# A perceiver layer on one core: one more slice in a seven-product down projection, and its products moved behind the next slice's gate and up products

## The chip, the cores and the metric

One core of a Trainium2 chip runs the whole program in one launch. The metric is the device time of an execution in microseconds (us). TensorE is called PE in the profile, VectorE DVE, ScalarE ACT, GpSimd POOL, and SyncE, which here only issues transfers, SP.

## The reference

The layer has three blocks on 256 tokens of width 512: cross attention with sigmoid scores over a context of 25088 tokens, causal self attention with 16 heads, and a feed-forward block. All is fp32. Only the last one is touched:

```
gu = x @ shared_gate_up_w
shared = _silu(gu[:, :Is]) * gu[:, Is:] @ shared_down_w
shared = shared * jax.nn.sigmoid(x @ shared_gate_w)
...
w, idx = jax.lax.top_k(probs, TOP_K)
...
act = _silu(gu_e[..., :I]) * gu_e[..., I:]
out_e = jnp.einsum('eci,eih->ech', act, expert_down_w)
...
return (y + shared).reshape(B, S, H)
```

The shared expert's inner width is 1024, an expert's 256; each token goes to 8 of 64 experts, weighted.

## The kernel before

**Stages.** Cross attention runs over 66 groups of context tokens and takes most of the time; self attention and the feed-forward block follow. In the last one the shared expert is cut into four slices ("s", 0) to ("s", 3) of inner width 256, so that a slice has the shape of an expert: gate and up weights of 512 x 512, down weights of 256 x 512. After the slices come the eight experts with most tokens, ("e", 0) to ("e", 7), each on all 256 tokens, and smaller work for experts with few tokens.

**One slice or expert.** gate_up (L1205) makes two PSUM banks by gate_up_products (L1187): 8 matmuls 128x256 for the gate, 8 for the up half. Sigmoid on ScalarE and two multiplies on VectorE (L1216 to L1218) make the hidden values hT, 256 x 256. down (L1347) then multiplies hT with the down weights, in one of two ways:

- Plain: for each of two token tiles two matmuls 128x512 (L1356), and one VectorE operation (L1365) that multiplies the result by the tokens' weights and adds it to what is summed so far: x2 (the residual) for ("s", 0), which thereby starts y, and y itself for the others.
- By seven products: the members of SEVEN (L803), which are slices 1 to 3 and experts 0 to 6, have their hT multiplied by the token weights first (L1220; a row of weights, broadcast to all partitions). hT and the down weights are each seen as 2 x 2 blocks. Four sums of blocks of hT are made on VectorE (S) and four of blocks of the weights on GpSimd (T), both at L1283 in sums_for_seven; then seven matmuls 128x256 (L1299 in down_by_seven), which go into two pairs of PSUM banks kept from the first member to the last. The first member starts the accumulation and the last one ends it; then add_seven (L1310) forms y from the seven totals in eleven VectorE operations.

**Order around the change.** run (L1369) issues gate_up of a slice, then down of the one before it, then what the table "between" has for this step: counted (token counts and the ranking of experts) after slice 0, load_first (weights of experts 0 to 2) after slice 1, permuted (the step pp, perm and pw_wt) after slice 2. So TensorE has: slice 0 gate and up, slice 1 gate and up, slice 0 down, slice 2 gate and up, slice 1 down, slice 3 gate and up, slice 2 down, slice 3 down, expert 0 gate and up. Between the two halves of slice 1's products, turn_weights (L1177) turns the token weights; GpSimd's queue stores them in DRAM (L1182) and reads one row back to all partitions (L1183), the row that slices multiply by. A scheduler orders the instructions of an engine, save those marked in_turn, which keep the program's order.

**Buffers and queues.** Weights of slices and experts share three buffers for gate and up and three for down (wpool), loaded through SP's queue, which waits in order: slice 3's take slice 0's, expert 0's take slice 1's, and so on. The S sums alternate between two rooms (the tiles x1 and x, no longer needed), by the member's place in SEVEN; the T sums have two buffers. Four PSUM banks, taken in turn by bank, serve gate and up halves, plain down products and the small matmuls of counted, turn_weights and permuted: each is used again four calls later.

Of the kernel before, what the change touches and what calls it, by code (L numbers as in the profile page):

```python
# [11 lines left out]
ALU = mybir.AluOpType  # L12
AX = mybir.AxisListType

P = 128
# [6 lines left out]
def tile_perceiver_layer(  # L22
# [25 lines left out]
    nc = tc.nc  # L48

    T, D = x.shape  # L50
# [10 lines left out]
    NI = I // P  # L61
# [445 lines left out]
    for i in range(2):  # L507
        t = cpool.tile([P, NT_SUMS, WIDTH + 2], F32, tag=f"T{i}", name=f"T_{i}", bufs=1)
# [174 lines left out]
    for line in RESULTS.strip().splitlines():  # L683
        to, x_, op, y_ = line.split()
        a_, b_, o_ = result(x_), result(y_), result(to)
        n = widths[to] = min(widths[x_], widths[y_])
        assert to not in ("c01", "c11") or n == WIDTH
        if to[0] == "c" and to[2] != "1":
            n = WIDTH - 2
# [83 lines left out]
    def bank(name):  # L773
        turns[1] += 1
        return apart(name) if turns[1] % 4 == 0 else among_three(name)
# [15 lines left out]
    NS = IS // I  # L791
    WHOLE = 8
# [6 lines left out]

    SEVEN = [("s", k) for k in range(1, NS)] + [("e", k) for k in range(WHOLE - 1)]  # L803
    weights = {}
    scales = {}
    late = ctx.enter_context(tc.tile_pool(name="late", bufs=1))
# [28 lines left out]
    def spread(tile_, row):  # L835
        return tile_.unsqueeze(1), weights_of_tokens[row, :].partition_broadcast(P)

    def load_expert(k, gu=None, dn=None, by=SP):
# [16 lines left out]
        queue.dma_start(dn, e_down[bass.ds(e, 1)].rearrange("o (c p) f -> p (o c) f", p=P))  # L855
        if ("e", k) in SEVEN:
            sc = scales["e", k] = scale_rooms[1 + k % 3]
# [73 lines left out]
    x2 = late.tile([P, NT, D], F32, tag="x2", name="x2")  # L931
# [200 lines left out]
    wsh = wt[:, :, E : E + 1]  # L1132
# [44 lines left out]
    def turn_weights():  # L1177
        pt = bank("pt_wt")
        for t in range(NT):
            nc.tensor.transpose(pt[0 : E + 1, t * P : (t + 1) * P], wt[:, t, :], ident)  # L1180
        nc.vector.tensor_copy(wT, pt[0 : E + 1, :T])
        nc.gpsimd.dma_start(weights_of_tokens, wT)  # L1182
        nc.gpsimd.dma_start(*spread(scale_rooms[0], slice(E, E + 1)))  # L1183
        for k in range(1, NS):
            scales["s", k] = scale_rooms[0]

    def gate_up_products(n, halves, lo, hi, mark=lambda ins: ins):  # L1187
        gu, _ = weights[n]
        for half, ph in enumerate(halves):
            if half > 0 and n == SEVEN[0]:  # L1190
                turn_weights()
            for f in range(NI):
                col = half * I + f * P
                for c in range(ND):
                    mark(
                        nc.tensor.matmul(  # L1196
                            ph[:, f * T + lo : f * T + hi],
                            lhsT=gu[:, c, col : col + P],
                            rhs=fT[:, c, lo:hi],
                            start=(c == 0),  # L1200
                            stop=(c == ND - 1),
                        )
                    )

    def gate_up(n, tiles_done=None):  # L1205

        nm = f"{n[0]}{n[1]}"
        if tiles_done is None:
            halves = [bank(f"ph_{nm}_{half}") for half in range(2)]
            gate_up_products(n, halves, 0, T)  # L1210
        else:
            halves = tiles_done
        pg, pu = halves
        hT = hidden.tile([P, NI, T], F32, tag="hT", name=f"hT_{nm}")
        hf = hT.rearrange("p f t -> p (f t)")
        nc.scalar.activation(hf, pg, AF.Sigmoid)  # L1216
        nc.vector.tensor_mul(hf, pg, hf)
        nc.vector.tensor_mul(hf, pu, hf)  # L1218
        if n in SEVEN:
            nc.vector.tensor_mul(hT, hT, scales.pop(n).unsqueeze(1).to_broadcast([P, NI, T]))  # L1220
            sums_of[n] = sums_for_seven(n, hT)
        return hT

# [20 lines left out]
        "p2 s3 b11",  # L1246
    )
    SUMS_OF_SEVEN = """
        y00 y00 + p0
        u1 p0 + p5  # L1250
        y00 y00 + p1
        u3 u1 + p4
        y01 y01 + u3
        y01 y01 + p2
        u2 u1 + p6
        u0 u2 - p3
        y10 y10 + u0
        u3 u2 + p4
        y11 y11 + u3
    """  # L1260
    HALF = D // 2
    sums_of = {}
    seven = []

    def block(n, hT, dn, s, t, nm):
        i, k = nm[1:2], nm[2:3]
        if nm[0] == "a":
            return hT[:, int(k), int(i) * P : (int(i) + 1) * P]
        if nm[0] == "b":
            return dn[:, int(i), int(k) * HALF : (int(k) + 1) * HALF]  # L1270
        return (s if nm[0] == "s" else t)[:, int(i), :]

    def sums_for_seven(n, hT):
        _, dn = weights[n]

        where = "x" if SEVEN.index(n) % 2 else "x1"
        s_ = act.tile([P, 4, P], F32, tag=where, name=f"s_{n[0]}{n[1]}")
        t_ = work.tile([P, 4, HALF], F32, tag="tokT", name=f"t_{n[0]}{n[1]}")
        for engine, text in ((nc.gpsimd, T_OF_SEVEN), (nc.vector, S_OF_SEVEN)):
            for line in text.strip().splitlines():  # L1280
                to, x_, op, y_ = line.split()
                f = engine.tensor_add if op == "+" else engine.tensor_sub
                made = f(*(block(n, hT, dn, s_, t_, nm) for nm in (to, x_, y_)))  # L1283
                if engine is nc.gpsimd:
                    in_turn(made)
        return s_, t_

    def product_of_seven(nm):
        i = int(nm[1])
        return seven[i // 4][:, i % 4 // 2, i % 2 * HALF : (i % 2 + 1) * HALF]  # L1290

    def down_by_seven(n, hT):
        _, dn = weights.pop(n)
        s_, t_ = sums_of.pop(n)
        if not seven:
            seven.extend(banks(f"seven_{i}") for i in range(2))
        for text in PRODUCTS_OF_SEVEN:
            nm, lhs, rhs = text.split()
            nc.tensor.matmul(  # L1299
                product_of_seven(nm),  # L1300
                lhsT=block(n, hT, dn, s_, t_, lhs),
                rhs=block(n, hT, dn, s_, t_, rhs),

                start=(n == SEVEN[0] and nm in ("p0", "p3", "p4", "p6")),
                stop=(n == SEVEN[-1] and nm in ("p1", "p2", "p5", "p6")),
            )
        if n == SEVEN[-1]:
            add_seven()

    def add_seven():  # L1310
        u = work.tile([P, 4, HALF], F32, tag="tok", name="u_seven")
        p5 = u[:, 0, :]
        nc.scalar.copy(p5, product_of_seven("p5"))

        def named(nm):
            if nm[0] == "y":
                return y[:, int(nm[1]), int(nm[2]) * HALF : (int(nm[2]) + 1) * HALF]
            if nm[0] == "u":
                return u[:, int(nm[1]), :]
            return p5 if nm == "p5" else product_of_seven(nm)  # L1320

        for line in SUMS_OF_SEVEN.strip().splitlines():
            to, x_, op, y_ = line.split()
            f = nc.vector.tensor_add if op == "+" else nc.vector.tensor_sub
            f(named(to), named(x_), named(y_))
# [4 lines left out]
    first = [pair[:, half, :] for half in range(2)]  # L1330
    route(0)
    gate_up_products(("s", 0), first, 0, P, in_turn)
    transposed_tile(fT, fn, 1, "fn", 2, two=True)
    route(1)
    gate_up_products(("s", 0), first, P, T, in_turn)
    for t in range(NT):
        choose(t)
# [3 lines left out]
    y = late.tile([P, NT, D], F32, tag="y", name="y")  # L1341
# [5 lines left out]
    def down(n, hT, parts=WIDE_PARTS):  # L1347
        if n in SEVEN:
            down_by_seven(n, hT)
            return  # L1350
        _, dn = weights.pop(n)
        nm = f"{n[0]}{n[1]}"
        for t, lo, hi in parts:
            pd = bank(f"pd_{nm}_{t}_{lo}")[:, 0 : hi - lo]
            for f in range(NI):
                nc.tensor.matmul(  # L1356
                    pd,
                    lhsT=hT[:, f, t * P : (t + 1) * P],
                    rhs=dn[:, f, lo:hi],
                    start=(f == 0),  # L1360
                    stop=(f == NI - 1),
                )
            w = wsh[:, t, :] if n[0] == "s" else wso[:, t, n[1] : n[1] + 1]
            so_far = x2 if n == ("s", 0) else y
            nc.vector.scalar_tensor_tensor(  # L1365
                y[:, t, lo:hi], pd, w, so_far[:, t, lo:hi], ALU.mult, ALU.add
            )

    def run(names, between, last=WIDE_PARTS):  # L1369

        pending = None
        for i, n in enumerate(names):
            hT = gate_up(n, first if n == ("s", 0) else None)
            if pending is not None:
                down(*pending)
            pending = (n, hT)
            if i in between:
                between[i]()
        down(*pending, last)


    order = late.tile([1, E], mybir.dt.int32, tag="order", name="order")
# [1 line left out]
    wso = late.tile([P, NT, E], F32, tag="wso", name="wso")  # L1384
# [261 lines left out]
    def remaining(lo):  # L1646
# [33 lines left out]
        last=LAST_PARTS,  # L1680
# [66 lines left out]
```

## Time and profile before

| | us |
|---|---|
| median of three runs | 778.94 |
| lowest and highest | 778.67, 779.83 |
| the profiled execution | 778.86 |
| its span (first to last instruction) | 777.1 |
| PE busy, DVE busy, POOL busy in it | 766.2, 557.9, 184.5 |

The profiled execution's own time is 1.76 us longer than its span. The granted PE clock was 0.999 of full speed. The feed-forward block's slices lie between 622 us and 661 us of the span.

How to read it: the profile has one row for each instruction that an engine ran, with the start (us from the span's start), the length, the line of the kernel and the tiles it wrote and read. An fp32 matmul of the program is two rows. "PEld" are the weight loads, which overlap the matmuls. The chain that ended last follows the work back from the last instruction, at each step to what released it. A DMA's time to landing runs from its issue until its data are there. An engine's wait is idle time of that engine, put down to what ended it.

### The profile page before, as it was taken

The numbers are of one execution on the slowest core, as the hardware profiler recorded it, in microseconds if no ns is written. First come the engines' busy times: TensorE is split into PE (matmuls) and PEld (weight loads), VectorE is DVE, ScalarE is ACT, GpSimd is POOL, SyncE is SP. The second block draws the span as 40 slices with busy tenths as digits, with TensorE's granted clock in tenths as the row PEclk, the third lists the DMA queues.
The fourth block names the chain that finished last, engine by engine and source line by source line (L and its number), as shares of the span: only waits on it lengthen the run. The fifth ranks groups of instructions, "written<-read, shape, count | busy, mean of one in ns | idle before, by whom it ended". The sixth has DMA issues, their size and how long they took to land.

```text
span 777.1 us, 12400 instructions
## 1 busy us (share of the span) xinstructions
PE 766.2 (99%) x4072; PEld 623.7 (80%) x4072; DVE 557.9 (72%) x1638; ACT 201.4 (26%) x486; POOL 184.5 (24%) x346
## 2 busy tenths in 40 slices
PE   8999999999999999999999999999999999999996
PEld 5888888888888888888888888888676588887574
DVE  5978878878888788788788888887756583523223
ACT  4222222222222222222222222222345320110110
POOL 3222322222223223222222232232123032131200
PEclk9999999999999999999999999999999999999999
DMA  9999999999787787787887887850430043599600
GB/s 251 284 233 249 256 237 272 232 225 216 180 208 181 188 206 176 203 200 173 207 194 168 213 190 184 211 134 2 138 107 2 0 145 102 165 323 390 233 1 31
DMA packets 154902, 141.98 MB, mean 183 GB/s; under 512 B 9238, under 2 KB 114339, under 8 KB 154832
## 3 DMA queue, kind: packets, MB, share of 16 engines
q1 hardware_dynamic: 154000, 140.41, 71.0%
q8 instruction: 34, 0.56, 0.3%
q10 hardware_dynamic: 672, 0.52, 0.2%
q0 software_dynamic: 160, 0.20, 0.2%
q14 instruction: 36, 0.29, 0.1%
HBM read 140.52 MB, written 0.59 MB: 182 GB/s over the span
## 4 chain that ended last, share of the span: by engine, by line
PE 96%; DVE 2%; ACT 0%; DMA 0%; POOL 0%; issue 0%; ACTq 0%
PE xacc L579 37%; PE pk L360 22%; PE pz L378 11%; PE ph_e L1196 7%; PE seven L1299 4%; PE ph_s L1196 3%; PE pw L941 2%; PE pa L877 2%; PE ph_few L1571 1%; PE ps L967 1%; PE ptp L1018 1%; PE po_few L1602 1%; PE pf L1548 1%; PE py L738 1%; PE pd_few L1616 1%; DMA x_sb<-in_x 0%
## 5 line engine op out<-in xcount | busy, mean ns | idle before, releaser
L579 PE MATMUL xacc<-T,S 128*128 128x172 f32 (+2 forms) x912 | 185.5, 308 | 0.0
L360 PE MATMUL pk<-cT,wkT_sb 128*128 128x384 f32 x512 | 175.5, 486 | 0.0
L579 PEld LDWEIGHTS xacc<-T,S 128*128 128x128 f32 x912 | 152.7, 190 | 20.3
L360 PEld LDWEIGHTS pk<-cT,wkT_sb 128*128 128x128 f32 x512 | 97.2, 190 | 54.3
L546 POOL TENSOR_TENSOR T<-ctx 128x172 f32<-128x172 f32 x65 | 31.7, 487 | 385.4 <-PE xacc L579 379.7
L324 DVE STREAM_TRANSPOSE cT<-quarters 128x1536 f32<-128x1536 f32 x64 | 113.2, 1770 | 0.2 <-issue 0.2
L546 DVE TENSOR_TENSOR T<-ctx 128x172 f32<-128x172 f32 (+1 forms) x262 | 113.3, 433 | 0.0
L546 DVE TENSOR_TENSOR S<-zT 128x128 f32<-128x128 f32 x196 | 56.2, 287 | 72.5 <-ACT zT L387 72.5
L378 PE MATMUL pz<-qT,kT 128*128 128x256 f32 x392 | 106.1, 379 | 0.7 <-ACT kT L369 0.7
L387 ACT ACTIVATE zT<-pz 128x256 f32<-128x256 f32 (+1 forms) x131 | 64.1, 489 | 114.1 <-PE pz L378 114.1
L579 PE MATMUL xacc<-T,zT 128*128 128x173 f32 (+1 forms) x396 | 90.0, 309 | 0.0
L579 PE MATMUL xacc<-ctx,S 128*128 128x172 f32 x392 | 78.5, 309 | 0.0
L369 ACT ACTIVATE kT<-pk,bk 128x384 f32<-128x384 f32 (+1 forms) x66 | 38.0, 577 | 147.0 <-PE pk L360 147.0
L546 DVE TENSOR_TENSOR S<-zT,S 128x128 f32<-128x128 f32 x325 | 76.1, 283 | 0.0
L556 ACT COPY T<-ctx 128x170 f32<-128x170 f32 (+1 forms) x130 | 43.1, 333 | 125.5 <-PE xacc L579 121.2
L546 POOL TENSOR_TENSOR T<-ctx,T 128x170 f32<-128x170 f32 (+1 forms) x130 | 72.3, 574 | 2.2 <-PE xacc L579 2.2
L378 PEld LDWEIGHTS pz<-qT,kT 128*128 128x128 f32 x392 | 68.6, 190 | 4.8 <-ACT kT L369 1.3
L546 DVE TENSOR_TENSOR T<-ctx,T 128x172 f32<-128x172 f32 x195 | 65.5, 361 | 8.2 <-PE xacc L579 1.5
L579 PEld LDWEIGHTS xacc<-T,zT 128*128 128x128 f32 x396 | 66.4, 190 | 0.1
L579 PEld LDWEIGHTS xacc<-ctx,S 128*128 128x128 f32 x392 | 62.8, 190 | 0.0
L579 PE MATMUL xacc<-ctx,zT 128*128 128x170 f32 (+1 forms) x264 | 59.5, 307 | 0.0
L1196 PE MATMUL ph_e<-fT,gu 128*128 128x256 f32 x256 | 57.8, 381 | 0.3 <-DVE rank L1504 0.3
(281 smaller groups left out, 770.0 us busy)
## 6 DMA issues: line engine op xcount, KB each, us to landing
ctx<-in_context SPq DMA_DIRECT2D x65, 768.0 KB, 5.4
quarters<-in_context SPq DMA_DIRECT2D x256, 192.0 KB, 6.5
gu<-in_e_gate_up SPq DMA_DIRECT2D x12, 1024.0 KB, 8.9
dn<-in_e_down SPq DMA_DIRECT2D x11, 512.0 KB, 6.8
gu_s<-in_s_gate_up SPq DMA_DIRECT2D x8, 512.0 KB, 6.2
a_wqT<-in_a_wqT SPq DMA_DIRECT2D x1, 2048.0 KB, 13.3
a_wout<-in_a_woutT SPq DMA_DIRECT2D x1, 2048.0 KB, 10.3
dn_s<-in_s_down SPq DMA_DIRECT2D x4, 512.0 KB, 8.1
```

Source lines behind the costliest of these rows:

```text
L324: in_turn(nc.vector.transpose(new_turned(g), q.rearrange("p b (c r) -> p c b r", r=R)))
L360: nc.tensor.matmul(pk, lhsT=w[:, c, :], rhs=cT[:, c, 0 : n // R, :].rearrange("p b r -> p (b r)"), start=(c == 0), stop=(c == ND - 1),)
L369: in_turn(nc.scalar.activation(kT[:, 0:n], pk, AF.Identity, bias=bk_sb))
L378: nc.tensor.matmul(pz[:, i * T : (i + 1) * T], lhsT=kT[:, at : at + P], rhs=qT, start=True, stop=True,)
L387: nc.scalar.activation(zT[:, blocks[0] : blocks[-1] + 1, :].rearrange("p j t -> p (j t)"), pz[:, 0 : len(blocks) * T], AF.Sigmoid, scale=1 ...
L546: in_turn(f(o_, a_, b_))
L556: in_turn(nc.scalar.copy(named[to][:, 0:n], named[x_][:, 0:n]))
L579: nc.tensor.matmul(banks_of_products[i][:, cols], lhsT=named[lhs], rhs=named[rhs][:, 0:n],  start=i not in opened, stop=(g == G - 1 and last),
L877: nc.tensor.matmul(pa[:, 0 : hi - lo], lhsT=a_wqT_sb[:, c, e * P : (e + 1) * P], rhs=anT[:, c, lo:hi], start=(c == 0), stop=(c == ND - 1),)
L941: nc.tensor.matmul(pw[t], lhsT=oT[:, e, t * P : (t + 1) * P], rhs=a_wout_sb[:, e, :], start=(e == 0), stop=(e == NE - 1),)
L1196: nc.tensor.matmul(ph[:, f * T + lo : f * T + hi], lhsT=gu[:, c, col : col + P], rhs=fT[:, c, lo:hi], start=(c == 0), stop=(c == ND - 1),)
L1299: nc.tensor.matmul(product_of_seven(nm), lhsT=block(n, hT, dn, s_, t_, lhs), rhs=block(n, hT, dn, s_, t_, rhs),  start=(n == SEVEN[0] and ...
```

## The change

Slice 0 becomes a member of SEVEN: its hT is multiplied by the row of token weights, and it takes the seven products in place of the four plain matmuls and the two updates of y. Since that row exists only after slice 1's gate and up products have begun, slice 0's multiply and sums are made after slice 1's own (weigh), and run holds slice 0's products back: no down is issued after slice 1's gate and up, and both slice 0's and slice 1's are issued after slice 2's. The final sums read x2 where they read y, since no plain product starts y any more. Slice 0 is now the member that starts the accumulation.

```diff
-    SEVEN = [("s", k) for k in range(1, NS)] + [("e", k) for k in range(WHOLE - 1)]
+    SEVEN = [("s", k) for k in range(NS)] + [("e", k) for k in range(WHOLE - 1)]
...
-        for k in range(1, NS):
+        for k in range(NS):
             scales["s", k] = scale_rooms[0]
...
-            if half > 0 and n == SEVEN[0]:
+            if half > 0 and n == ("s", 1):
                 turn_weights()
...
-        if n in SEVEN:
-            nc.vector.tensor_mul(hT, hT, scales.pop(n).unsqueeze(1).to_broadcast([P, NI, T]))
-            sums_of[n] = sums_for_seven(n, hT)
+        if n in SEVEN and n != ("s", 0):
+            weigh(n, hT)
         return hT
+
+    def weigh(n, hT):
+        nc.vector.tensor_mul(hT, hT, scales.pop(n).unsqueeze(1).to_broadcast([P, NI, T]))
+        sums_of[n] = sums_for_seven(n, hT)
...
-        y00 y00 + p0
+        y00 x00 + p0
...
-        y01 y01 + u3
+        y01 x01 + u3
...
-        y10 y10 + u0
+        y10 x10 + u0
...
-        y11 y11 + u3
+        y11 x11 + u3
...
-            w = wsh[:, t, :] if n[0] == "s" else wso[:, t, n[1] : n[1] + 1]
-            so_far = x2 if n == ("s", 0) else y
+            w = wso[:, t, n[1] : n[1] + 1]
...
-        pending = None
+        pending = []
         for i, n in enumerate(names):
             hT = gate_up(n, first if n == ("s", 0) else None)
-            if pending is not None:
-                down(*pending)
-            pending = (n, hT)
+            if n == ("s", 1):
+
+                weigh(*pending[0])
+            else:
+                for each in pending:
+                    down(*each)
+                pending = []
+            pending.append((n, hT))
             if i in between:
                 between[i]()
-        down(*pending, last)
+        for each in pending:
+            down(*each, last)
```

More of the change, by code (lines that the diff above doesn't have):

```diff
@@ L1315, in named @@
         def named(nm):
-            if nm[0] == "y":
-                return y[:, int(nm[1]), int(nm[2]) * HALF : (int(nm[2]) + 1) * HALF]
+            if nm[0] in "xy":
+                return (x2 if nm[0] == "x" else y)[:, int(nm[1]), int(nm[2]) * HALF : (int(nm[2]) + 1) * HALF]
             if nm[0] == "u":
@@ L1362, in down @@
                 )
-            w = wsh[:, t, :] if n[0] == "s" else wso[:, t, n[1] : n[1] + 1]
-            so_far = x2 if n == ("s", 0) else y
+            w = wso[:, t, n[1] : n[1] + 1]
             nc.vector.scalar_tensor_tensor(
-                y[:, t, lo:hi], pd, w, so_far[:, t, lo:hi], ALU.mult, ALU.add
+                y[:, t, lo:hi], pd, w, y[:, t, lo:hi], ALU.mult, ALU.add
             )
     def run(names, between, last=WIDE_PARTS):
-        pending = None
+        pending = []
         for i, n in enumerate(names):
             hT = gate_up(n, first if n == ("s", 0) else None)
-            if pending is not None:
-                down(*pending)
-            pending = (n, hT)
+            if n == ("s", 1):
[5 more added lines that the diff above has]
+            pending.append((n, hT))
             if i in between:
                 between[i]()
-        down(*pending, last)
+        for each in pending:
+            down(*each, last)
     order = late.tile([1, E], mybir.dt.int32, tag="order", name="order")
```

## Prediction

> **What bounds the kernel now.** I read the page first: busy time by engine, then the chain that ended last.
>
> ```profile
> PE 766.2 (99%) x4072; PEld 623.7 (80%) x4072; DVE 557.9 (72%) x1638; ACT 201.4 (26%) x486; POOL 184.5 (24%) x346
> ...
> PE 96%; DVE 2%; ACT 0%; DMA 0%; POOL 0%; issue 0%; ACTq 0%
> ```
>
> TensorE is never idle and the chain lies on it: 96% of the span. So a microsecond of TensorE work that disappears is a microsecond of time, provided nothing else becomes late. Next, the same chain in order of time around the edit (start, length, what):
>
> ```profile
> 626.71 3.22 PE ph_s L1196 x14
> 629.93 0.22 PE pt_wt L1180 x2
> 630.15 3.46 PE ph_s L1196 x16
> 633.61 3.43 PE pd_s L1356 x8
> 637.04 6.91 PE ph_s L1196 x32
> 643.95 3.02 PE seven L1299 x14
> 646.97 0.25 PE pp L1433 x2
> ```
>
> Here pd_s is slice 0's down product, ph_s at 637.04 slice 2's gate and up, seven at 643.95 slice 1's down by seven products. TensorE goes from one to the next without a gap. Each fp32 matmul of the program is two rows (four matmuls give x8, seven give x14). Last, the timeline of VectorE and GpSimd in the stretch where the moved work will land:
>
> ```profile
> 637.57 0.14 DVE L1422 CAST active<-left 1x1 int32<-1x1 f32 x1
> 637.60 0.73 POOL L1283 TENSOR_TENSOR t_s<-dn_s,t_s 128x256 f32<-128x256 f32 x1
> 637.64 0.73 DVE L1365 SCALAR_TENSOR_TENSOR y<-pd_s,wt,x 128x512 f32<-128x512 f32 x1
> 638.29 1.27 POOL L1283 TENSOR_TENSOR t_s<-dn_s 128x256 f32<-128x256 f32 x1
> 638.30 0.67 DVE L1220 TENSOR_TENSOR hT_s<-hT_s,wqT 128x512 f32<-128x512 f32 x1
> 639.00 1.44 DVE L1283 TENSOR_TENSOR s_s<-hT_s 128x128 f32<-128x128 f32 x2
> 639.52 0.77 POOL L1283 TENSOR_TENSOR t_s<-t_s,dn_s 128x256 f32<-128x256 f32 x1
> ...
> 645.43 0.50 DVE L1283 TENSOR_TENSOR s_s<-hT_s 128x128 f32<-128x128 f32 x2
> ```
>
> The same pair of small sums took 0.50 us with GpSimd idle and 1.44 us beside it; GpSimd's add took 1.27 instead of 0.72 when VectorE's multiply of two SBUF operands started beside it. So these two engines take turns.
>
> **The change part by part.**
>
> *Products (removed and added).* Four matmuls 128x512 go (3.43 us), seven 128x256 come (3.02 us, by slice 1's row): **-0.41 us** of TensorE, all on the path. Nothing else on TensorE changes but its order.
>
> A rule against this is in the Trainium skill, "TensorE: Matmul & The Clock Gate", section on the back-to-back issue gap: a sustained stream of weight load and matmul costs 81 ns at 128 columns and 131 ns at 512. Interpolated (my estimate) that is 98 ns at 256, and fourteen short rows would cost 1.31 times eight long ones: +1.1 us instead of -0.41. The trace disagrees: 3.02/14 = 0.216 us and 3.43/8 = 0.429 us, proportional to the columns.
>
> *Order.* Slice 2's gate and up moves up to 633.61 and ends 6.91 later, at 640.52; slice 0's seven products follow, then slice 1's to 646.56, where before they ended at 646.97. What each start needs:
>
> - Slice 2's weights were requested with the first three slices, long before. Its two PSUM banks are now those of the token counts (read at 626.75) and of slice 1's gate half (read by 631.6): free.
> - Slice 1's products start 0.41 us earlier behind a longer queue; their operands are made before slice 0's. No wait.
> - Slice 0's products need its hidden values weighed, four S sums (VectorE) and four T sums (GpSimd). This is the tight place.
>
> *The tight place.* Before, TensorE's weight load for the first of the seven stood at 643.57; it now falls at 643.57 - 3.43 = 640.14, with 0.43 us (3.02/7) per product: the third product (needs the last T sum) at 641.00, the fourth (first S sum) at 641.43, the next at 641.86, 642.29, 642.72. VectorE is busy to 637.71 as before. It loses two y updates (0.73 each, off the path) and gains one multiply (0.67) and four sums. GpSimd does slice 0's T sums in the four places that slice 2's had, 636.80 to 640.29. The program's order on VectorE: weigh slice 1, weigh slice 0, then the sums: three of slice 1, the first of slice 0, the last of slice 1, three of slice 0. Taking turns: GpSimd to 638.33; weigh 1 to 638.97; GpSimd to 639.56 (as its 1.27 row did); weigh 0 to 640.2; GpSimd's last to 640.85; first sum to about 640.95. Then GpSimd has nothing ready, since slice 2's T sums need a buffer that slice 1's products hold, and sums follow at 0.21 ((645.85 - 645.43)/2 in slice 2's row): the fourth, slice 0's first, at 641.6. Against the needs: 640.2 for 640.14, 640.85 for 641.00, 641.6 for 641.43. TensorE waits about 0.1 and then up to **0.2 us in all**; the later sums, at 642.0, 642.2 and 642.4, are in time. Bounds of this wait, which no row shows: below 0 is excluded, since TensorE is already without gaps; 0 if the turns fall better; 0.9 if one more turn of 0.72 comes ahead of the fourth sum (641.6 + 0.72 - 641.43). I take 0.2, by the nearest rows.
>
> *Scale row.* The multiply waits for the row broadcast that GpSimd issues at 633.35; it lands 4.1 us later in the profile, at 637.45, before VectorE wants it (637.64). Before, it could come 3 us late without harm; now the slack is 0.75 us with a turn of GpSimd's between the two multiplies (640.14 - 2 x 0.67 - 0.6 = 638.2) and 1.35 without one (638.8).
>
> *Queues.* SP: slice 3's down weights reuse slice 0's buffer. Before, they went out at 637.07, when pd_s ended; now when slice 0's seven end, about 643.7. Behind them on SP stand expert 0's down weights, which wait for slice 1's products (647.09 before, about 646.9 now), so nothing is held longer. Slice 3's weights landed 4.8 us after issue, the slowest of the four slices 9.5: 648.5 to 653.2. They are needed by slice 3's T sums, for which GpSimd is free at about 649.3 (646.62 - 0.2, and four adds of 0.72); they end at 652.2, or 656.1 with the slowest landing, and TensorE wants them at about 658: cover 2 us or more. GpSimd: slice 2's T sums move from 636.80 to about 646.4, used from 655; slice 3's follow, as said. VectorE: slice 2's S sums now wait for slice 0's products (shared room), about 643.5; behind them stands the permutation step (647.26 before), for which they end by about 645. ScalarE's sigmoid of slice 2 moves with its product. Cost of all these: 0; if the cover failed, a wait as long as the lateness.
>
> *The end.* The final sums read x2 where they read y: the same eleven operations. After 646.97 the chain has two VectorE links, 0.85 us at 668 and 0.48 at the end; both follow TensorE and move with it.
>
> **Sum.** -0.41 + 0.2 = -0.2 us. The profiled execution took 778.86 (span 777.1, 1.76 around it): **778.6 us**. The median of the three runs is 0.08 above it. I call a difference under 0.2% (1.6 us) no change, about what a measurement of this kernel can tell.
>
> **A second look at the sums.** The Trainium skill, "VectorE: DVE Perf Modes", section on the DRAIN that can't be avoided, says that a next operation starts only once the pipe has emptied, save where it is not held. If no sum were let in early, three steps of 0.29 instead of 0.21 would put the fourth sum 0.24 later and the total near 0. The starts 0.21 apart in the profile speak for the faster figure.
>
> **Rivals.**
>
> 1. *Forecast*: gain kept in part or whole, wait 0 to 0.4: 778.4 to 778.85. Chance 0.76.
> 2. *A wait takes the gain's place*: VectorE and GpSimd share more badly than counted, TensorE waits 0.4 to 0.9 at slice 0's first or fourth product: 778.85 to 779.35 (778.86 - 0.41 + the wait). For it: margins of 0.1; against it: GpSimd runs out of work at 640.85. Chance 0.17.
> 3. *Slower: the scale row comes late.* Place: TensorE's first seven-product load. From a landing after 638.8 each microsecond is one of time; it passes the gain at 639.2 and 0.2% at 640.8, 7.4 us after issue. The slowest row of that DRAM tile landed after 10.5: 643.85, then 5.05 us of wait less 0.41, 783.5. Against it: 4.1 here, and expert 0's load, which goes out at 634.20 in both versions, is all it competes with. Chance 0.05.
> 4. *The change saves more than its products*, over 1.6 us: the only gaps left are the 0.85 and 0.48 us links, which it does not touch. Chance 0.02. That it saves nothing, because seven products cost as much as four, is excluded by the two rows.
>
> **How the numbers follow.** Likeliest 778.6. The range runs from the lowest run less the whole gain (778.67 - 0.41, about 778.2) to the upper wait with a high run, 779.6; it leaves out the tails (779.83 - 0.41 + 0.2 = 779.6). Faster by over 0.2%: 0.02; within: 0.93; slower: 0.05.
>
> **What would show it.** In the profile after: no pd_s row for slice 0; seven x28 in one piece of 6.04 us starting near 640.5; a TensorE wait of 0.1 to 0.3 us on VectorE there; the step pp at 646.6 to 646.9; slice 3's down weights issued near 643.7 and no TensorE wait at 658. Wrong: a wait of a microsecond or more at 640, or any new wait on a DMA.

## The result and the profile after

| | before | changed |
|---|---|---|
| median of 22 runs each (us) | 778.85 | 779.97 |
| profiled execution (us) | 778.86 | 780.41 |
| its span | 777.1 | 778.6 |

The changed kernel takes 1.0014 times as long (95% interval 1.0008 to 1.0020): 1.1 us slower. That is within the 0.2% that the prediction called no change, but on the other side of 1 than forecast and above its range (779.6).

The page of the changed kernel, TensorE's row and the shares of the chain that ended last:

```profile
PE 766.4 (98%) x4078; PEld 624.4 (80%) x4078; DVE 558.8 (72%) x1641; ACT 201.4 (26%) x486; POOL 189.8 (24%) x350
...
PE 17%; DVE 0%; issue 0%
```

TensorE's chain, 96% of the span before, is followed back for only 17%, and there it breaks off. The list of TensorE's waits (who waited for whom: us, times, longest) names the place:

```profile
PE seven L1301 <- POOL t_s L1285: 1.2, 1, 1.2
```

GpSimd's busy time rose by 5.3 us (184.5 to 189.8), while four adds of 0.72 us explain 2.9. The timeline of the changed kernel shows the rest (start, length, engine, line, what):

```profile
637.95 0.14 DVE L1429 CAST active<-left 1x1 int32<-1x1 f32 x1
637.98 3.51 POOL L1285 TENSOR_TENSOR t_s<-dn_s,t_s 128x256 f32<-128x256 f32 x1
638.01 1.27 DVE L1223 TENSOR_TENSOR hT_s<-hT_s,wqT 128x512 f32<-128x512 f32 x2
639.22 0.47 DVE L1285 TENSOR_TENSOR s_s<-hT_s 128x128 f32<-128x128 f32 x2
...
640.63 0.27 DVE L1285 TENSOR_TENSOR s_s<-hT_s,s_s 128x128 f32<-128x128 f32 x1
640.83 0.67 DVE L1216 TENSOR_TENSOR hT_s<-ph_s,hT_s 128x512 f32<-128x512 f32 x1
641.46 0.72 POOL L1285 TENSOR_TENSOR t_s<-dn_s 128x256 f32<-128x256 f32 x1
642.14 0.72 POOL L1285 TENSOR_TENSOR t_s<-t_s,dn_s 128x256 f32<-128x256 f32 x1
...
642.91 0.30 PEld L1301 LDWEIGHTS seven<-t_s,hT_s 128*128 128x128 f32 x2 [1.57 <-POOL t_s L1285]
```

The second of slice 0's T adds, started at 637.98, took 3.51 us instead of 0.73. Beside it VectorE ran its two multiplies and eight sums in a row, 638.01 to 640.90, none held up; GpSimd's add got through only when VectorE had come to an operation that reads PSUM (L1216, from 640.83; the add ended at 641.49). The last T add ended at 642.86, and the weight load of slice 0's third product waited for it, 1.57 us. TensorE's chain from there:

```profile
642.87 0.04 issue
642.91 5.45 PE seven L1301 x24
648.36 0.25 PE pp L1440 x2
```

The step pp, which ends the affected stretch, began at 646.97 before. Single executions also differ ahead of the change; VectorE's row "active" measures that: 637.57 before, 637.95 here, 0.38 us. So the change itself costs 648.36 - 646.97 - 0.38 = +1.01 us. I use this difference, "pp moved", for every run below; it is free of what happens elsewhere. (In e2 and e11, where the edit itself moves VectorE's row, I take the start of pt_wt, 629.93 before.)

The cost is made up of two parts. TensorE stood idle for 1.17 us (the 1.2 of the list; its weight load, which runs ahead, had waited 1.57), and the 24 rows behind the wait took 5.45 us, 0.27 more than 24 x 0.216. Together that is 1.44 us, which the 0.41 us saved brings down to about the +1.01 measured.

### The profile page after: what moved, and what is told of

It reads as the page before. It is cut to its first block, busy times and chain, and to the rows that moved or that the text cites. A ratio compares the mean times of both kernels' runs of the same rounds, so it can differ in the third digit from the quotient of the medians.

```text
span 778.6 us, 12420 instructions
## 1 busy us (share of the span) xinstructions
PE 766.4 (98%) x4078; PEld 624.4 (80%) x4078; DVE 558.8 (72%) x1641; ACT 201.4 (26%) x486; POOL 189.8 (24%) x350
## 5 line engine op out<-in xcount | busy, mean ns | idle before, releaser
(279 smaller groups left out, 777.9 us busy)
```

## Experiments

Three theories stood at the start. **P**: VectorE's unbroken run of operations with two SBUF operands shuts GpSimd out. ("The port" below is a name for whatever the two engines share on the way to SBUF; the runs show what it does, not what it is.) **S**: VectorE has too much to do. **D**: putting the products off costs by itself, through buffers and transfers. Ratios are to the kernel before in the same series, with the 95% interval.

| run | edit to the changed kernel | pp moved, us | ratio |
|---|---|---|---|
| changed | | +1.01 | 1.0014 [1.0008, 1.0020] |
| e9_same_order | repeat, order by hand | +1.02 | 1.0013 [1.0003, 1.0022] |
| e1_t0_first | slice 0's T sums first | -0.39 | 0.9994 [0.9984, 1.0003] |
| e2_early | slice 0's T sums at 606 us | -0.42 | 0.9998 [0.9989, 1.0007] |
| e3_order | T products last | -0.42 | 0.9993 [0.9984, 1.0002] |
| e12_slice1_first | slice 1's products first | -0.42 | 0.9993 [0.9982, 1.0004] |
| e8_breaks | three memsets | -0.39 | 0.9991 [0.9982, 1.0001] |
| e14_one_break | one memset | -0.42 | 0.9988 [0.9975, 1.0000] |
| e13_later_start | one copy ahead of the run | -0.42 | 0.9992 [0.9983, 1.0001] |
| e10_swap_order | e1 and e3 | -0.44 | 0.9988 [0.9978, 0.9999] |
| e11_early_order | e2 and e3 | -0.42 | 0.9993 [0.9982, 1.0005] |
| e7_no_s_sums | slice 0's S sums left out | +0.06 | 1.0001 [0.9991, 1.0010] |
| e6_more_sums | slice 0's S sums twice | +0.62 (see text) | 1.0027 [1.0018, 1.0037] |
| e4_put_off | (kernel before) put off alone | -0.01 | 0.9999 [0.9990, 1.0008] |
| e5_join | joined, not put off | +6.57 | 1.0080 [1.0054, 1.0107] |

### The T sums of slice 0 ahead of slice 1's (e1)

```diff
         if n in SEVEN and n != ("s", 0):
+            if n == ("s", 1):
+                t_sums(("s", 0))
             weigh(n, hT)
```

(t_sums holds the loop over T_OF_SEVEN, taken out of sums_for_seven, which now makes only those not made yet.)

> The changed kernel with one swap: GpSimd makes slice 0's four T sums before slice 1's; work and number of instructions are the same. Theory P (port): TensorE's new wait of 1.6 us at slice 0's third product comes from GpSimd's second add for slice 0 (3.51 us in place of 0.72), shut out by VectorE's unbroken run of ten operations with two SBUF operands. With the swap slice 0's T sums end before that run begins and slice 1's, held in its place, are needed 1.7 us later or more: the wait goes, 0.4 us under the kernel before (778.4 to 778.6). Theory S (VectorE's extra sums are what is late): as the changed kernel, 1.1 us over before. Theory D (putting the products off costs by itself, by buffers and transfers that start later): as the changed kernel, 1.1 over.

Measured: median 778.62 (before 778.99). GpSimd is still shut out, but now it is slice 1's second add:

```profile
638.37 3.52 POOL L1299 TENSOR_TENSOR t_s<-dn_s,t_s 128x256 f32<-128x256 f32 x1
```

and TensorE goes through all 28 rows of both slices without a wait:

```profile
641.30 6.04 PE seven L1312 x28
647.34 0.25 PE pp L1451 x2
```

The work on every engine is the same and one order is changed, which speaks against S and D. The gain, 0.39 by pp, is about the forecast's 0.41.

### The product order (e3)

```diff
-        "p3 a11 t3",
         "p4 s0 t0",
+        "p2 s3 b11",
         "p5 s1 t1",
         "p6 s2 t2",
-        "p2 s3 b11",
+        "p3 a11 t3",
```

(with start and stop flags moved to the first and last product of each bank)

> The changed kernel with the seven products of every member in another order: p0 p1 p4 p2 p5 p6 p3, so that the last T sum is wanted by the last product and not by the third. GpSimd stays shut out for as long. Theory P: in the changed kernel's trace the T sums end at about 641.5, 642.1 and 642.9, and TensorE would now want them at 642.2, 642.7 and 643.1: wait under 0.3 us, time 0.1 to 0.4 under before. Theory S: the first S sum is wanted 0.43 earlier and the last one 0.86 earlier: no better than the changed kernel, 1.1 over before or more. Theory D: 1.1 over.

Measured: 778.49 (before 778.99). The add still took 3.52 us, from 637.76, and TensorE did not wait. So S falls twice: the S sums are wanted earlier here and come in time.

### Put off alone (e4)

The kernel before, with run's list of held-back products but slice 0's plain down.

```diff
-            if pending is not None:
-                down(*pending)
-            pending = (n, hT)
+            if n != ("s", 1):
+                for each in pending:
+                    down(*each)
+                pending = []
+            pending.append((n, hT))
...
```

> One part of the change alone: the kernel before, with slice 0's plain down products put off until after slice 2's gate and up products, slice 0 not joining the seven. Theory P: no new GpSimd or VectorE work, no wait: the time of before within 0.2 us. Theory D: the cost of putting off shows here, up to 1.5 us over before.

Measured: 778.81 (before 778.99), pp moved by -0.01. D falls: putting off makes slice 3's down weights later and costs TensorE nothing.

### Breaks in VectorE's run (e8, e9)

The order that the scheduler had chosen was written out by hand, so that memsets could be set into it:

```diff
+        def gap():
+            if made[0] < 3:
+                in_turn(nc.vector.memset(breaks[:, made[0], :], 0.0))
+                made[0] += 1
...
+        for k in (1, 0):
+            hT = hTs["s", k]
+            in_turn(nc.vector.tensor_mul(hT, hT, scale.unsqueeze(1).to_broadcast([P, NI, T])))
+            gap()
...
+            if at == 1:
+                gap()
```

The memsets stand behind slice 1's multiply, behind slice 0's, and behind the second sum.

> The changed kernel, same order on every engine, with three VectorE operations added that read nothing from SBUF (memsets 128x64): behind slice 1's multiply, behind slice 0's multiply and behind the second sum. Theory P, in its narrow form (an unbroken run of two-operand operations keeps the port, any break gives it to GpSimd): GpSimd gets a turn at each break, its adds take about 1.3 us instead of 3.5, T sums end near 641; VectorE's sums come about 2 us later, so that TensorE waits some 0.3 us for the first S sum: 0 to 0.3 under before, although there is more work. Theory P in its wide form (GpSimd is held off while VectorE works on SBUF at all): three more operations make it later still, 1.2 to 1.6 over before. Theory S: more VectorE work, 1.2 to 1.6 over before.

Measured: 778.34 (before 778.99), with three instructions more. Slice 0's adds took 1.30, 1.17 and 0.77 us and ended at 641.03; no wait on TensorE at all. The control, the same code without memsets:

> The changed kernel again: written so that VectorE's run is in the program's order by hand, with every engine's instructions in the very order of the changed kernel and no memset. It is the control of the kernel with three memsets and a repeat of the changed kernel. Theory P: the 3.5 us add and a TensorE wait of 1.6 us are there again, 1.1 over before (0.9 to 1.3).

Measured: 779.91 (before 779.02); the add took 3.52 us, TensorE waited 1.2 again. So the memsets do it, not the hand-written order. That an operation with one operand in PSUM does not hold GpSimd off can be seen in the kernel before, in the rows at 637.60 and 637.64 that the prediction shows: GpSimd's add and the y update (L1365) ran side by side and took 0.73 us each.

### Fewer and more sums (e7, e6)

```diff
...
+        if n == ("s", 0):
+            s_ = sums_of["s", 1][0]
         for engine, text in ((nc.gpsimd, T_OF_SEVEN), (nc.vector, S_OF_SEVEN)):
+            if n == ("s", 0) and engine is nc.vector:
+                continue
```

> The changed kernel without slice 0's four S sums: the products that need them read slice 1's, so this part of the computation is left out. GpSimd's order and work stay. Theory P, narrow: VectorE's unbroken run is four operations (0.82 us) shorter, GpSimd's second add for slice 0 takes about 2.7 us in place of 3.5, and TensorE waits about 0.75 us at slice 0's third product in place of 1.57: 0.3 us over before. If GpSimd's add were slow by itself: 3.5 us, 1.1 over before.

Measured: 778.59 (before 779.02), pp moved +0.06. The timeline of the kernel without these sums:

```profile
637.91 2.50 POOL L1291 TENSOR_TENSOR t_s<-dn_s,t_s 128x256 f32<-128x256 f32 x1
...
639.55 0.27 DVE L1291 TENSOR_TENSOR s_s<-s_s,hT_s 128x128 f32<-128x128 f32 x1
639.86 0.71 DVE L1291 TENSOR_TENSOR s_s<-hT_s,s_s 128x128 f32<-128x128 f32 x1
```

2.50 us instead of 3.51: one sum sooner than expected, since the last sum had to wait for the one ahead of it (639.82 to 639.86), and in that gap of 0.04 us GpSimd got in. TensorE's weight load waited 0.61 us, where 0.75 was expected.

```diff
-        for engine, text in ((nc.gpsimd, T_OF_SEVEN), (nc.vector, S_OF_SEVEN)):
+        twice = S_OF_SEVEN * 2 if n == ("s", 0) else S_OF_SEVEN
+        for engine, text in ((nc.gpsimd, T_OF_SEVEN), (nc.vector, twice)):
...
```

> The changed kernel with slice 0's four S sums made twice (same values, VectorE works 0.82 us longer in its run). Theory P, narrow: GpSimd's second add for slice 0 takes about 4.3 us, TensorE waits about 2.4 us: 1.9 over before. If GpSimd's add were slow by itself: 3.5 us, 1.1 over before, unless TensorE then waits for VectorE, which the profile would name.

Measured: 781.02 (before 779.02), ratio 1.0027, or 2.1 us: the 1.9 of theory P lies within the interval. But no profile shows the add of 4.3 us, since the one execution that was profiled (780.12, the lowest of ten) went another way:

```profile
638.84 0.73 POOL L1288 TENSOR_TENSOR t_s<-dn_s 128x256 f32<-128x256 f32 x1
638.88 2.37 DVE L1223 TENSOR_TENSOR hT_s<-hT_s,wqT 128x512 f32<-128x512 f32 x2 [0.61 <-DMA wqT<-weights_of_tokens]
...
639.52 1.18 POOL L1288 TENSOR_TENSOR t_s<-t_s,dn_s 128x256 f32<-128x256 f32 x1
```

Here the row of token weights landed late. VectorE started at 638.88 while GpSimd's adds were under way and had to wait (2.37 us for two multiplies that took 1.27 in the changed kernel), and GpSimd then got its next turn between the two multiplies, although there is no break there. TensorE's waits in this execution were on VectorE. So P as first put could not be the whole rule, and three of the 22 runs of the changed kernel (777.74, 777.83, 777.93; the next is 779.08) also showed no lost time. A second form, **Q**: a run keeps the port only if its first operation found it free.

### Who comes first (e13, e14)

The edit is to the hand-written order without memsets (e9):

```diff
+        in_turn(nc.vector.tensor_copy(breaks[0:1, 0, 0:1], active))
         for k in (1, 0):
             hT = hTs["s", k]
```

> The changed kernel's orders with one VectorE copy of a single element behind the last operation before the run, so that the run starts some 0.17 us later and GpSimd's second add for slice 0 is at the port first. Theory P as first put (an unbroken run keeps the port to its end): the second add takes 0.73, the third is shut out for the rest of the run, the last T sum comes at the same 642.9 and TensorE waits 1.4 us: 1.0 to 1.2 over before. Theory Q (a run keeps the port only if its first operation found it free; an operation that had to wait for GpSimd is followed by a turn of GpSimd's): the engines take turns as the prediction had it, adds of 0.7 to 1.3, wait under 0.3: 0.1 to 0.4 under before. By Q a difference of 0.1 us in the start decides over 1.4 us, which would account for the three of 22 runs of the changed kernel that took 777.7 to 777.9.

Measured: 778.43 (before 778.96). The run is the same ten operations, unbroken; it only starts 0.19 us later after "active" than in the changed kernel (638.18 - 637.93 against 638.01 - 637.95):

```profile
637.97 0.72 POOL L1284 TENSOR_TENSOR t_s<-dn_s,t_s 128x256 f32<-128x256 f32 x1
...
638.11 0.14 DVE L1306 CAST breaks<-active 1x1 f32<-1x1 int32 x1
638.18 2.19 DVE L1309 TENSOR_TENSOR hT_s<-hT_s,wqT 128x512 f32<-128x512 f32 x2
638.65 1.17 POOL L1284 TENSOR_TENSOR t_s<-dn_s 128x256 f32<-128x256 f32 x1
639.79 1.17 POOL L1284 TENSOR_TENSOR t_s<-t_s,dn_s 128x256 f32<-128x256 f32 x1
640.29 1.01 DVE L1293 TENSOR_TENSOR s_s<-hT_s 128x128 f32<-128x128 f32 x2
641.23 0.28 DVE L1293 TENSOR_TENSOR s_s<-s_s,hT_s 128x128 f32<-128x128 f32 x1
```

GpSimd's second add is at the port before VectorE and takes 0.72; VectorE's two multiplies then take 2.19 together, with an add between them, and the adds end at 640.96. The engines take turns. TensorE:

```profile
640.87 6.04 PE seven L1329 x28
646.91 0.25 PE pp L1468 x2
```

An operation on one element takes the whole loss away. P as first put falls; it went as Q had it. One memset of the three (the edit is to e8), behind slice 1's multiply, gives the same:

```diff
-            if made[0] < 3:
+            if made[0] < 1:
```

> The changed kernel's orders with one memset alone, behind slice 1's multiply. Theory P as first put: the second add gets in at that break (1.3 us), the third is shut out by the nine operations left, the last T sum comes at about 642.9: 1.0 to 1.2 over before. Theory Q: behind the break slice 0's multiply has to wait for GpSimd, and turns follow without further breaks: wait under 0.4, 0 to 0.4 under before.

Measured: 778.39 (before 778.96), adds of 1.29, 1.17 and 0.77, no wait on TensorE:

```profile
637.65 1.29 POOL L1284 TENSOR_TENSOR t_s<-dn_s,t_s 128x256 f32<-128x256 f32 x1
637.68 0.67 DVE L1308 TENSOR_TENSOR hT_s<-hT_s,wqT 128x512 f32<-128x512 f32 x1
638.32 0.11 DVE L1303 MEMSET breaks<- 128x64 f32 x1
638.36 1.14 DVE L1308 TENSOR_TENSOR hT_s<-hT_s,wqT 128x512 f32<-128x512 f32 x1
638.91 1.17 POOL L1284 TENSOR_TENSOR t_s<-dn_s 128x256 f32<-128x256 f32 x1
```

Q was put after e6's profile and foretold both of these runs; P as first put failed in both. The starts in the profile do not by themselves tell who was first at the port: in the changed kernel GpSimd's row begins 0.03 us ahead of VectorE's and in e14 too, yet VectorE's multiplies were not held up there (1.27 us for two, 0.67 for the first). When VectorE started 0.21 us behind (e13), GpSimd's add went first.

### Other ways to mend it (e2, e12, e10, e11), and the other part alone (e5)

Slice 0's T sums were taken out into t_sums and called ahead of the first slice's products:

```diff
+    t_sums(("s", 0))
     pair = banks("ph_first")
```

> The changed kernel with slice 0's T sums, which need nothing but its down weights, issued on GpSimd before the routing, where it is idle (from 606 to 631 in the changed kernel's trace). Slice 1's four stay where they are, and end before VectorE's run. Theory P: no wait of TensorE at 640; 0.4 under before, unless the early adds hold up VectorE's layer norm there (one add of two SBUF operands at 611.4, at most one turn of 0.7 us, with little slack). Theory D: 1.1 over.

Measured: 778.41 (before 779.02). The early adds took 0.73 each from 605.76 to 608.66; no wait on TensorE came of them. The ratio, 0.9998, says less than the profile (pp moved -0.42).

```diff
-    SEVEN = [("s", k) for k in range(NS)] + [("e", k) for k in range(WHOLE - 1)]
+    SEVEN = [("s", k) for k in (1, 0, 2, 3)] + [("e", k) for k in range(WHOLE - 1)]
...
-                for each in pending:
+                for each in reversed(pending):
```

> The changed kernel with the two held-back down products exchanged on TensorE: slice 1's seven products, whose T sums end before VectorE's run, then slice 0's. GpSimd stays shut out for 3.5 us, but slice 0's last T sum (642.9 in the changed kernel's trace) is then wanted at about 644. Theory P: no wait, 0.4 under before. A rival (slice 3's down weights, which now go out only after slice 0's products, about 3 us later than in the changed kernel, come too late): a new wait of TensorE on a transfer or on GpSimd near 658.

Measured: 778.48 (before 778.93). Slice 3's weights were late for GpSimd,

```profile
647.49 0.72 POOL L1285 TENSOR_TENSOR t_s<-dn_s 128x256 f32<-128x256 f32 x1 [1.03 <-DMA dn_s<-in_s_down]
```

but not for TensorE.

> Both mendings at once: slice 0's T sums ahead of slice 1's on GpSimd, and the product order p0 p1 p4 p2 p5 p6 p3. Each alone took the wait away whole, so together they give no more than either: 0.4 under before (778.3 to 778.7).

> Slice 0's T sums in GpSimd's idle time before the routing, and the product order p0 p1 p4 p2 p5 p6 p3. As the version with the early sums alone: 0.4 to 0.6 under before.

Measured: 778.49 and 778.47 (before 778.93): as either alone. The mended versions lie 0.37 to 0.65 us under before by their medians and 1.3 us or more under the changed kernel. Against the kernel before, only e10's interval lies wholly below 1; the profiles, where pp stands 0.39 to 0.44 us earlier in all nine, carry the claim that they beat it.

```diff
             if n == ("s", 1):

                 weigh(*pending[0])
-            else:
-                for each in pending:
-                    down(*each)
-                pending = []
-            pending.append((n, hT))
+            for each in pending:
+                down(*each)
+            pending = [(n, hT)]
```

> The other part of the change alone: slice 0 joins the seven but its products are not put off; the scheduler sets them between the two halves of slice 2's. TensorE would want the first of them at about 636.7, and its hidden values are weighed at 639.3 at the earliest (the row of token weights lands at 637.5 to 638), the last T sum comes at 642.9: waits of 2.6 and 2.8 us, less 0.41: 4 to 5.5 us over before. If the row did not matter: at or under before.

Measured: 785.81 (before 778.93). TensorE waited 1.9 us for the weighed values and 2.4 us for the T sum, as expected in kind; most of the rest is a lower clock, shown at the end. Joining without putting off loses much more than it saves.

## Why the prediction was wrong

**Products, -0.41: right.** 28 rows in 6.04 us, and pp moved by -0.39 to -0.44 in every version in which slice 0 joins the seven and TensorE does not wait. The rule on short matmuls from the Trainium skill did not bear here; the rows decided rightly.

**Order, queues and the end: right.** No wait on slice 2's weights or banks, none on slice 1's products. Slice 3's down weights were issued at 645.42 (forecast 643.7, later by the wait ahead of it) and landed 3.4 us later; GpSimd waited 0.8 for them and TensorE not at all. e4 confirms that putting off is free. From pp to the end of the last y update both kernels take 124.4 us.

**The tight place: right place, wrong mechanism and size.** The step that failed is "Taking turns: GpSimd to 638.33; weigh 1 to 638.97; GpSimd to 639.56", and with it "**0.2 us in all**" and the upper bound of 0.9, which allowed for one more turn. There were no turns: VectorE had the port from 638.01 and kept it for ten operations, and GpSimd's add took 3.51 us in place of 0.72 (that VectorE came first is inferred from the lengths, as said under e14). The wait cost 1.01 + 0.41 = 1.42 us where 0.2 was put down. "A wait of a microsecond or more at 640" was the prediction's own sign of being wrong. That the last T sum, not the first S sum, would be late follows from the same error: slice 0's first S sum ended 1.5 us earlier than forecast (640.09, not 641.6), and the last T sum 2.0 us later (642.86, not 640.85), both in an execution that ran 0.38 us late from the start.

**Why the rows misled.** The turns were read from stretches before in which VectorE's operations either had a gap of 0.03 us between them (638.97 to 639.00, waiting for a result) or had waited for GpSimd themselves. The new run has neither: sums of two independent slices stand interleaved, 0.20 us apart. In e13, with the start moved by 0.19 us, the turns came as forecast: the last T sum ended at 640.96 against 640.85, in an execution that ran 0.36 us late. Even the 0.2 us wait was not there.

**The scale row.** It landed in time in the changed kernel's profile (issued 633.71, 3.9 us). In e6's execution it was late (5.0 us), and there it seems to have helped, since GpSimd could finish first: that execution was the lowest of the ten. Rival 3, with one price for lateness, had not thought of that.

**The sums and the pipe.** The slower case of the second look, in which no sum is let in early, was rightly not taken: the sums started 0.20 us apart. But just this closeness left GpSimd no gap.

**Rivals.** The second rival, a wait in the gain's place through VectorE and GpSimd, is what came, at another product and 0.5 us above its range; it had been given 0.17.

**Left open.** That the three runs of the changed kernel at 777.7 to 777.9 are executions in which GpSimd came first at the port is likely after e13 (the two starts lie 0.03 us apart in the profile) but no profile of such a run was taken. Why an operation that had to wait gives the next turn away is not known.

## What to carry to other kernels

When work is added to VectorE beside GpSimd, ask whether its operations with two SBUF operands will stand in a row without a gap, and who starts first: in these runs a run that started on a free port held GpSimd off to its end (3.51 us for an add of 0.72), so that the price was the length of the run, not a turn. Put GpSimd's operations that need only early data ahead of such a run (e1, e2), or order their consumer last (e3); then it no longer matters who comes first. A bound for an unseen wait should take the whole run that could stand in the way, not one more of its steps.

## What the hardware showed unexpectedly

**One element decides 1.4 us.** A copy of a single value, or one memset of 0.11 us, takes TensorE's wait away (e13, e14). The Trainium skill, "GPSIMD Engine Reference", section Specifications, says that GpSimd's SBUF interfaces are shared with VectorE and contend with its operations with two SBUF inputs; the runs agree, and show what it can cost here: 3.51 us for an add of 0.72, held off through ten operations.

**The clock between two waits.** In e5, the stretches of TensorE (us: busy with instructions for PE, PEld, DVE, ACT, POOL, then the granted clock, DMA share and GB/s):

```profile
639.00:640.00 1.00, 0.78 (x4) 0.68 (x4) 1.00 (x6) 0.00 (x0) 1.00 (x1) 1.00 0.60 231
640.20:640.30 0.10, 0.10 (x1) 0.00 (x0) 0.10 (x1) 0.00 (x0) 0.10 (x1) 0.90 0.06 21
640.30:640.40 0.10, 0.05 (x1) 0.00 (x0) 0.10 (x2) 0.00 (x0) 0.10 (x1) 0.50 0.00 0
646.00:647.00 1.00, 1.00 (x4) 0.82 (x3) 0.00 (x0) 0.00 (x0) 0.29 (x1) 0.50 0.00 0
647.10:647.20 0.10, 0.10 (x2) 0.06 (x2) 0.00 (x0) 0.00 (x0) 0.10 (x1) 0.97 0.00 0
648.00:650.00 2.00, 2.00 (x11) 1.74 (x11) 0.00 (x0) 0.00 (x0) 1.61 (x3) 1.00 0.77 194
```

TensorE waited 1.9 us up to 639.22 and 2.4 us up to 642.79, with four rows between. The granted clock fell to 0.50 at about 640.28, while the last of these rows was still running: the first wait alone lay behind it, and the second had not begun. It stayed there until about 647.1, though TensorE worked again from 642.79; the last ten rows of slice 0's products took 4.54 us instead of 10 x 0.216 = 2.16. The measured waits less the 0.41 saved give 3.9 us, and with these 2.4 it is 6.3 of the 6.57 by which pp moved. The single wait of 1.2 us in the changed kernel left the clock at 1.00. The Trainium skill, "TensorE: Matmul & The Clock Gate", section on what is actually happening, states a half clock after an idle window of some 3.4 us and a full one after a busy one of that length. The 4.3 us of work from 642.79 to 647.1 are of that size, but no wait here was that long: a wait of 1.9 us came ahead of the fall. How long a wait has to be, and whether it matters when it comes, is not known from these runs.
